# Second attention: folding three of four denominators with accumulating DMAs, and moving an exp table load

## The chip, the cores and the metric

One Trainium2 chip, one core. The time is that of the device, in microseconds, for one execution of the whole program; of several executions the median is given. Profiles come from one execution, taken by the hardware profiler.

## What is computed

Input `x` has shape (16, 256, 32, 32): 16 batches, 256 channels, 1024 positions. All data are float32. The reference, cut to what matters:

```python
# layer 0: attention with 4 heads of 64
xs  = x.reshape(B, C, S).transpose(0, 2, 1)
qkv = xs @ w_proj + b_proj
attn = softmax(q k^T * 64**-0.5) ; res = attn @ v
x = (res @ w_out + b_out + xs)            # residual
# layer 1: group norm, attention with 8 heads of 32, group norm, MLP
xn  = group_norm(x, gn1)
q, k, v = split(xn @ qkv_w.T)             # 8 heads of 32
attn = softmax(q k^T * 32**-0.5 + phys_bias) ; out = attn @ v
x = x + out @ proj_w.T + proj_b
h = gelu(mlp_w1 @ group_norm(x, gn2) + b1) ; x = x + mlp_w2 @ h + b2
```

A softmax is computed without subtracting a maximum: the exponentials are weighted with v and summed, and the result is then multiplied by the inverse of the sum of the exponentials, the denominator. The bias of a head is a constant, so its exponential is a factor: it is multiplied into the weights of v (`scale_v`, L209) and into the ones that sum the denominators (`eones`, L202).

## The kernel before, in words

The 16 batches are pipelined. For each batch the program first runs the attention of layer 0 (`attention_a`), then the hidden layer of the MLP of the batch before (`mlp`, its list `hidden`), then the attention of layer 1 (`attention_b`), and between the steps of `attention_b` it places pieces of other work: the second half of q, k, v of this attention, the projections of the next batch's first attention, and the output products of the last MLP (`fill`, L1134 to L1155).

Layouts: keys or channels lie on the 128 partitions, 512 queries (`TB`) along the free axis. `attention_b` (L508) has four items: two blocks of queries times two groups of four heads of 32, in the order of L513. An item has eight blocks of 128 keys, taken two at a time, so a step (`units`, L515) is one pair. A step computes scores for four heads and two key blocks (`scores`, L518: 16 matmuls of 32 rows by 64 columns, L532), exponentials on ScalarE (L547), on VectorE the running sum of the exponentials over the key blocks (`add`, L553, tiles `es`, two per item with two heads each, L563), and for the step before the products with v (`weigh`, L579, L584), whose result goes to `res` by ScalarE or VectorE (L595, L597).

After the last key block of an item, the sums still lie on 128 partitions, each head with 128 x 512 values. `normalise` (L601) sums over the partitions on TensorE: four matmuls of 128 rows by 32 columns (L606), one for each head, with 512 queries each. The float32 matmul is two passes, so the profile shows eight records. Each head's denominator then stands on 32 partitions. `denominators` (L357) copies them to SBUF (L358), spreads 4 x 512 values over 128 partitions by a DMA (L363), inverts them (L367), writes them to DRAM (L368) and broadcasts them back with four DMAs (L373); `scale` (L629) multiplies `res` by them, and for the second group of heads issues the projection (`out_proj`).

The order is written out by hand. Each engine runs its own instructions in the order in which they were emitted, apart from small moves by the scheduler. `Later` (L31) holds functions due after a number of ticks; the driver `run` (L1036) ticks once a step, before the step's pieces, except past the last step. The numbers in `later.after(n, ...)` are such ticks: a denominator is due at the tick of the step that weighs the item's last pair (L599), its inverse one tick later, its use one more. In `run_pieces` (L1045) each piece is followed by a tick.

PSUM has three wide tiles of two banks (`wide`, L297), handed out least recently used first, and two single banks (`bank`, L303). The scores of the first key block of a step take both single banks; `weigh` takes bank 0 and the denominators bank 1. `aside` (L307) lends a single bank to a piece of q, k or v at the start of `attention_b`.

q, k and v of `attention_b` come from `qkv` (L769): TensorE products, copied to SBUF by ScalarE (L782 for q and k, L800 for v). ScalarE uses one table set for Exp and another for Gelu, so its table is loaded at the first Gelu of a batch (L919) and at the first Exp after it (L547).

At the start of the program GpSimd loads the MLP weights, forms sums of them and keeps them in DRAM (`make_blocks`, L148). Later it has the small sums of denominators and inverses (L369, L370), which at the end decide whether all of them were in range, and one power per group norm (L746). SP issues all other DMAs.

Of the kernel before, what the change touches and what calls it, by code (L numbers as in the profile page):

```python
# [8 lines left out]
F32 = mybir.dt.float32  # L9
I32 = mybir.dt.int32  # L10
AF = mybir.ActivationFunctionType
ALU = mybir.AluOpType
AX = mybir.AxisListType

P = 128
# [3 lines left out]
HEADS1, D1 = 8, 32  # L19
TB = 512  # L20
# [34 lines left out]
def kernel(  # L55
# [21 lines left out]
    nc = tc.nc  # L77
# [8 lines left out]
    const = ctx.enter_context(tc.tile_pool(name="const", bufs=1))  # L86
# [113 lines left out]

    ebias = const.tile([P, HEADS1], F32, name="ebias")
    eones = const.tile([P, HEADS1, D1], F32, name="eones")  # L202

    def exp_bias():
        nc.scalar.activation(ebias, pb, AF.Exp)
        nc.vector.tensor_copy(eones, ebias.unsqueeze(2).to_broadcast([P, HEADS1, D1]))


    def scale_v():  # L209
# [9 lines left out]
    with ExitStack() as first:  # L219
        first_pass(  # L220
            first, tc, x, out,
            dict(
                wp=wp, bqk=bqk, pb=pb, bo=bo, g1w=g1w, g1b=g1b, g2w=g2w,
                g2b=g2b, pjb=pjb, m1b=m1b, m2b=m2b, wo=wo, wq=wq, wpj=wpj,
                m2b2=m2b2, gavg=gavg, mhalf=mhalf, ones=ones, eones=eones,
                bvo=bvo, at_start=at_start, load_rest=load_rest, exp_bias=exp_bias,
                scale_v=scale_v,
                make_blocks=make_blocks,
                in_range=in_range,
            ),  # L230
        )
# [15 lines left out]
def first_pass(ctx, tc, x, out, k):  # L247
    nc = tc.nc
# [54 lines left out]
    def bank(name, n):  # L303
        return ps_a.tile([P, TB], F32, tag=f"b{n}", name=name)
# [4 lines left out]
    def single(name):  # L309
        return bank(name, aside.pop()) if aside else wide(name)[:, 0, :]  # L310
# [43 lines left out]

    def denominators(key, den, d, full, waits, then):  # L357
        nc.scalar.copy(d, den)  # L358
        n = full.shape[1]
        w = 4 * TB // P  # L360
        spread = work.tile([P, w], F32, tag="spread", name=f"sp_{key}", bufs=2)
        row = dram.tile([4 * TB // n, n], F32, tag="row", name=f"row_{key}", bufs=4)
        nc.sync.dma_start(spread, d[::32].rearrange("p (a b) -> p a b", b=w))  # L363

        def invert():
            inverse = work.tile([P, w], F32, tag="inverse", name=f"inv_{key}", bufs=2)
            tc.keep_in_program_order(nc.vector.reciprocal(inverse, spread))  # L367
            nc.sync.dma_start(row.rearrange("r (a b) -> (r a) b", b=w), inverse)  # L368
            nc.gpsimd.tensor_add(dsum, dsum, spread)  # L369
            nc.gpsimd.tensor_add(isum, isum, inverse)  # L370
            num = P * n // (4 * TB)
            for r in range(P // num):
                nc.sync.dma_start(  # L373
                    full[r * num : (r + 1) * num], row[r].partition_broadcast(num)
                )
            later.after(waits[1], lambda: then(full))

        later.after(waits[0], invert)
# [129 lines left out]
    def attention_b(b, qT, kT, v, project):  # L508
# [70 lines left out]
        def weigh(i, kb, es):  # L579
            t, c = items[i]  # L580
            acc = bank(f"acc_{key}_{i}_{kb}", 0)
            for m in range(2):
                for g in range(G):
                    nc.tensor.matmul(  # L584
                        acc[g * D : (g + 1) * D, :],
                        v[:, kb + m, c * G + g],
                        es[2 * m + g // 2][:, g % 2, :],
                        start=(m == 0),
                        stop=(m == 1),
                    )  # L590
            if t not in res:
                res[t] = result(t)
            r = res[t][c]
            if kb == 0:
                nc.scalar.copy(r, acc)  # L595
            else:
                nc.vector.tensor_add(r, r, acc)  # L597
            if kb == SB - 2:
                later.after(1, lambda: normalise(i, r, i == len(items) - 1))  # L599

        def normalise(i, r, last):  # L601
            t, c = items[i]
            at_end = last and b == B - 1
            den = bank(f"den_{key}_{i}", 1)
            for g in range(G):
                nc.tensor.matmul(  # L606
                    den[g * D : (g + 1) * D, :],
                    k["eones"][:, c * G + g],
                    sums[i][g // 2][:, g % 2, :],
                    start=True,  # L610
                    stop=True,
                )
            full = work.tile([P, TB], F32, tag="full", name=f"rd_{key}_{i}", bufs=1)
            if at_end:

                nc.vector.reciprocal(full, den)
                scale(i, r, last, full)
                for tot, what in ((dsum, den), (isum, full)):
                    part = small.tile([P, 1], F32, tag="part", name="part")
                    nc.vector.tensor_reduce(part, what, AX.X, ALU.add)  # L620
                    nc.gpsimd.tensor_add(tot[:, :1], tot[:, :1], part)
                return
            denominators(
                f"{key}_{i}", den, full, full,
                (3, 5) if last else (1, 1),
                lambda full: scale(i, r, last, full),
            )

        def scale(i, r, last, full):  # L629
            t, c = items[i]  # L630
            tc.keep_in_program_order(nc.vector.tensor_mul(r, r, full))
            if c == CC - 1:
                issue = project(t, res[t])
                if last and b + 1 < B:
                    handed.append(issue)
                else:
                    later.after(1, issue)
# [131 lines left out]
    def qkv(key, D, src, weights, b_qk, qT, kT, v_dst):  # L769
        def qk(ch, which, t):  # L770
            ps = single(f"qk_{key}_{ch}_{which}_{t}")
            for cc in range(CC):
                product(
                    ps,
                    weights(cc, which)[:, ch * P : (ch + 1) * P],
                    src[:, cc, t * TB : (t + 1) * TB],
                    start=(cc == 0),
                    stop=(cc == CC - 1),
                )
            d = (kT if which else qT)[:, ch, t * TB : (t + 1) * TB]  # L780
            if b_qk is None:
                nc.scalar.copy(d, ps)  # L782
            else:
                nc.scalar.activation(  # L784
                    d, ps, AF.Identity, bias=b_qk[:, which, ch : ch + 1]
                )

        def v(n):
            ps = single(f"v_{key}_{n}")
            for i in range(2):  # L790
                sb = 2 * n + i
                for cc in range(CC):
                    product(
                        ps[:, i * C : (i + 1) * C],
                        src[:, cc, sb * P : (sb + 1) * P],
                        weights(cc, 2),
                        start=(cc == 0),
                        stop=(cc == CC - 1),
                    )
            nc.scalar.copy(  # L800
                v_dst()[:, 2 * n : 2 * n + 2],
                ps.rearrange("p (b h d) -> p b h d", b=2, d=D),
            )

        return (
            [
                lambda ch=ch, which=which, t=t: qk(ch, which, t)
                for ch in range(CC) for which in (1, 0) for t in range(NT)
            ],
            [lambda n=n: v(n) for n in range(SB // 2)],  # L810
        )

# [82 lines left out]
    def mlp(b, xb):  # L895
# [44 lines left out]
            gelu(0, 1, i, ps[:, 1, :])  # L940

        def finish(i):
            ps = open_sums.pop(i)
            products_of(i, [(7, ps[:, 0, :], False), (6, ps[:, 1, :], False)])
            rest = gs[1, 1, i]
            nc.vector.tensor_add(unit(0, 0, i), rest, ps[:, 0, :])  # L946
            nc.vector.tensor_add(rest, rest, ps[:, 1, :])
            gelu(0, 0, i, gs[0, 0, i])
            gelu(1, 1, i, rest)
            combine((1, 0), (0, 0), False, i)  # L950
            combine((0, 1), (1, 1), False, i)

        hidden = [
            lambda part=part, i=i: part(i)
# [4 lines left out]
        def combine(to, what, plus, only=None):  # L959
            for i in range(n4) if only is None else (only,):  # L960
                d = gs[(*to, i)]
                (nc.vector.tensor_add if plus else nc.vector.tensor_sub)(  # L962
                    d, d, gs[(*what, i)]
                )
# [128 lines left out]

    later.after(2, fold_bias)
    later.after(8, k["scale_v"])
    hidden, outputs = [], []
    last = NT * CC * SB // 2 - 1
    for b in range(B):
# [379 lines left out]
```

## Time and profile before

| | |
|---|---|
| median of 3 runs | 3666.4 us (3664.72 to 3667.44) |
| profiled execution | 3666.7 us |
| its span, first to last instruction | 3664.9 us |
| mean granted TensorE clock | 0.999 |
| matmuls of the denominators, L606 | 512 records, 67.4 us busy |
| table loads at the first Exp, L547 | 15, 1283 ns each |
| table loads at the first Gelu, L919 | 16, 1283 ns each |
| DMA over the span | 138.36 MB, mean 38 GB/s |

A busy time is the union of the intervals of an engine's instructions. Matmuls overlap each other, since each of four tiles of the array works by itself, so the duration of one record (592 ns for 512 columns) says less than the distance between the starts of two groups. "PEld" is the loading of weights, which runs beside the matmuls. A row of the timeline has the start, the duration, the engine, the line, the operation, what it writes and reads, and its count; in brackets stands how long the engine had been idle before it and what ended that. DMAs appear under the queue that issues them (SPq, or POOL for GpSimd), with the time of the issue alone, not that of the transfer.

### The profile page before, as it was taken

What the parts mean: (1) busy time and instruction counts of PE and PEld (TensorE: products, weight loads), DVE (VectorE), ACT (ScalarE), POOL (GpSimd) and SP (SyncE); (2) the same over time, 40 slices, a digit from 0 to 9 for tenths busy, and PEclk for the clock granted to TensorE, in tenths of its full rate; (3) what the DMA queues carried; (4) which work ended last, traced back from release to release, by engine and by line L of the source; (5) the groups of instructions that cost most, each with busy time, mean ns of one, the idle gap of its engine ahead of it and who ended that gap; (6) DMA issues with size and microseconds to landing.
All of it is one profiled execution on the core that took longest, in us unless ns stands there. A gap on an engine that the chain in (4) does not pass through costs nothing.

```text
span 3664.9 us, 79373 instructions
## 1 busy us (share of the span) xinstructions
PE 3632.6 (99%) x34221; PEld 1346.2 (37%) x34221; DVE 2658.1 (73%) x3424; ACT 2154.3 (59%) x2832; POOL 129.5 (4%) x266
## 2 busy tenths in 40 slices
PE   9999999999999999999999999999999999999999
PEld 3433343333433334333343333434334343343433
DVE  4586777767777677776767777677777777767777
ACT  4665657556565655656556565564655656556572
POOL 3000000000000000000000000000000000000000
PEclk9999999999999999999999999999999999999999
DMA  4000110101101011010110101101011010100100
GB/s 147 10 17 29 55 33 14 51 30 54 33 14 51 30 54 33 14 51 31 53 33 20 51 27 51 33 19 50 27 51 33 19 50 29 50 33 31 47 28 27
DMA packets 66549, 138.36 MB, mean 38 GB/s; under 512 B 35630, under 2 KB 36398, under 8 KB 61966
## 3 DMA queue, kind: packets, MB, share of 16 engines
q1 hardware_dynamic: 63116, 126.64, 10.7%
q8 instruction: 270, 4.42, 0.5%
q0 software_dynamic: 1328, 6.17, 0.5%
q14 instruction: 89, 0.73, 0.1%
q10 hardware_dynamic: 1746, 0.40, 0.1%
HBM read 111.17 MB, written 21.23 MB: 36 GB/s over the span
## 4 chain that ended last, share of the span: by engine, by line
PE 91%; DVE 4%; ACT 3%; DMA 1%; issue 1%; SPq 0%; ACTq 0%; POOL 0%; DVEq 0%
PE s_a L398 12%; PE acc_b L584 12%; PE s_b L532 12%; PE acc_a L419 12%; PE m L344 10%; PE m L906 9%; PE qk_a L344 6%; PE qk_b L344 5%; PE v_a L344 3%; PE j L344 3%; PE v_b L344 2%; ACT e_b L547 2%; PE o L344 2%; PE den_b L606 1%; DVE g L962 1%
## 5 line engine op out<-in xcount | busy, mean ns | idle before, releaser
L563 DVE TENSOR_TENSOR es_b<-es_b,e_b 128x1024 f32<-128x1024 f32 x768 | 899.3, 1219 | 243.8 <-ACT e_b L547 243.8
L547 ACT ACTIVATE e_b<-s_b 128x1024 f32<-128x1024 f32 (+1 forms) x1280 | 982.9, 864 | 132.2 <-PE s_b L532 132.0
L406 ACT ACTIVATE e_a<-s_a 128x1024 f32<-128x1024 f32 x512 | 521.2, 1025 | 360.0 <-PE s_a L398 347.6
L398 PE MATMUL s_a<-q,k 64*64 64x512 f32 x4096 | 544.3, 593 | 0.0
L419 PE MATMUL acc_a<-e_a,v 64*64 64x512 f32 x4096 | 540.1, 589 | 0.0
L532 PE MATMUL s_b<-q,k 32*64 32x512 f32 x8192 | 519.7, 600 | 4.9 <-DVE res_b L597 1.6
L431 DVE TENSOR_TENSOR es_a<-es_a,e_a 128x1024 f32<-128x1024 f32 x384 | 473.9, 1234 | 64.8 <-ACT e_a L406 41.2
L584 PE MATMUL acc_b<-e_b,v 128*32 128x512 f32 x4096 | 492.1, 598 | 0.0
L344 PE MATMUL m<-g,w 128*32 128x512 f32 (+1 forms) x3320 | 404.3, 592 | 0.0
L532 PEld LDWEIGHTS s_b<-q,k 32*64 32x64 f32 x8192 | 170.9, 130 | 321.3 <-issue 130.9
L419 PEld LDWEIGHTS acc_a<-e_a,v 64*64 64x64 f32 x4096 | 187.9, 133 | 251.5 <-issue 218.4
L398 PEld LDWEIGHTS s_a<-q,k 64*64 64x64 f32 x4096 | 175.9, 133 | 246.7 <-issue 193.1
L563 DVE TENSOR_TENSOR es_b<-e_b,e_b 128x1024 f32<-128x1024 f32 x128 | 150.8, 1220 | 153.4 <-ACT e_b L547 153.4
L906 PE MATMUL m<-gn_h,w 128*128 128x512 f32 x512 | 243.7, 604 | 5.7 <-DVE g L932 3.3
L584 PEld LDWEIGHTS acc_b<-e_b,v 128*32 128x32 f32 x4096 | 108.5, 109 | 357.5 <-ACT e_b L547 194.7
L344 PE MATMUL qk_a<-x,wp 128*32 128x512 f32 (+1 forms) x1856 | 235.1, 593 | 4.1 <-ACT k L784 4.1
L344 PE MATMUL qk_b<-gn_g,wq 128*32 128x512 f32 (+1 forms) x1280 | 234.0, 592 | 0.0
L597 DVE TENSOR_TENSOR res_b<-res_b,acc_b 128x512 f32<-128x512 f32 x192 | 131.8, 686 | 129.8 <-PE acc_b L584 129.8
L344 PEld LDWEIGHTS m<-g,w 128*32 128x32 f32 (+1 forms) x3320 | 121.4, 112 | 262.3 <-issue 235.3
L962 DVE TENSOR_TENSOR g<-g,g 128x512 f32<-128x512 f32 x320 | 206.3, 681 | 4.0 <-ACT g L919 2.8
L906 PE MATMUL m<-hs,w 128*128 128x512 f32 x384 | 177.9, 592 | 0.1
L919 ACT ACTIVATE g<-g,m1b 128x512 f32<-128x512 f32 x128 | 92.2, 722 | 99.3 <-DVE g L946 72.2
(147 smaller groups left out, 2803.6 us busy)
## 6 DMA issues: line engine op xcount, KB each, us to landing
w<-w_kept SPq DMA_DIRECT2D x30, 1792.0 KB
d_a<-row_a SPq DMA_DIRECT2D x64, 256.0 KB
rd_b<-row_b SPq DMA_DIRECT2D x252, 64.0 KB
out_dram<-x SPq DMA_DIRECT2D x63, 256.0 KB
x<-in_x_dram SPq DMA_DIRECT2D x30, 512.0 KB
w_kept<-w_made POOLq DMA_DIRECT2D x2, 1792.0 KB, 6.0
w_made<-in_L_conv_mlp_w_dram POOLq DMA_DIRECT2D x8, 256.0 KB, 6.1
x<-in_x_dram SPq DMA_DIRECT2D x4, 256.0 KB
```

The lines of the kernel that those rows point to most:

```text
L344: nc.tensor.matmul(o[sl], w[:, sl], r, **flags)
L398: nc.tensor.matmul(s[h : h + HALF, g, :], kT[g * D : (g + 1) * D, c, kb * P + h : kb * P + h + HALF], qT[g * D : (g + 1) * D, c, t * TB : ...
L406: nc.scalar.activation(e, s, AF.Exp, scale=float(D) ** -0.5)
L419: nc.tensor.matmul(accs[i][h][g * D : (g + 1) * D, :], v[h * HALF : (h + 1) * HALF, kb, c * 2 + g], e[h * HALF : (h + 1) * HALF, g, :], st ...
L431: nc.vector.tensor_add(sums[i], held[i] if kb == 1 else sums[i], e)
L532: nc.tensor.matmul(outs[g][h : h + HALF, :], kT[g * D : (g + 1) * D, c, k0 : k0 + HALF], qT[g * D : (g + 1) * D, c, t * TB : (t + 1) * TB] ...
L547: nc.scalar.activation(to, s, AF.Exp, scale=float(D) ** -0.5)
L563: ins = nc.vector.tensor_add(d, es[n % 2] if kb == 0 else d, es[n])
L584: nc.tensor.matmul(acc[g * D : (g + 1) * D, :], v[:, kb + m, c * G + g], es[2 * m + g // 2][:, g % 2, :], start=(m == 0), stop=(m == 1),)
L597: nc.vector.tensor_add(r, r, acc)
L906: nc.tensor.matmul(ps, blocks[1][number - 1][:, i * P : (i + 1) * P], inputs[b][number], start=first, stop=True, skip_group_check=not first,)
L962: (nc.vector.tensor_add if plus else nc.vector.tensor_sub)(d, d, gs[(*what, i)])
```

## The change

It has three parts.

First, the denominators of the first three items of each `attention_b` are computed in another way; the last item keeps `normalise`. As soon as the sums of an item are complete, `fold` adds the four blocks of 32 partitions of each head's sums to one another. It does so in DRAM: SP writes the first block of 32 rows (two DMAs, one for each pair of heads), and GpSimd issues three rounds of two DMAs that add the other blocks onto it. One more DMA of GpSimd loads the result as `packed`, in which the 32 rows of four heads lie on 128 partitions. Two ticks later `normalise_folded` runs four matmuls on it, of 128 rows by 32 columns, each over 128 of the 512 queries. Their weights `folded` hold, for each head, its factor in the eight columns that belong to that head and zeros elsewhere, so one matmul gives all four heads. `fold_ones` makes them on GpSimd at the start. `denominators` gets an argument `parts` for the new layout; its broadcasts go out in pieces of 128 values rather than rows of 512.

Second, the first piece of v in `attention_b` is copied by VectorE rather than ScalarE.

Third, after the last hidden piece of the MLP a small Exp on 128 x 1 values is issued on ScalarE, two ticks later.

```diff
+    folded = const.tile([P, HEADS1 * D1 // P, D1], F32, name="folded")
...
+    def fold_ones():
+        nc.gpsimd.memset(folded, 0.0)
+        g_num = P // D1
+        w = D1 // g_num
+        for c in range(HEADS1 // g_num):
+            for g in range(g_num):
+                rows = slice(g * D1, (g + 1) * D1)
+                nc.gpsimd.tensor_copy(
+                    folded[rows, c, g * w : (g + 1) * w], eones[rows, c * g_num + g, :w]
+                )
...
-    def denominators(key, den, d, full, waits, then):
+    def denominators(key, den, d, full, waits, then, parts=1):
...
-        nc.sync.dma_start(spread, d[::32].rearrange("p (a b) -> p a b", b=w))
+        nc.sync.dma_start(
+            spread, d[:: 32 // parts].rearrange("p (a b) -> p a b", b=w)
+        )
...
-                nc.sync.dma_start(
-                    full[r * num : (r + 1) * num], row[r].partition_broadcast(num)
-                )
+                to, of = full[r * num : (r + 1) * num], row[r]
+                if parts > 1:
+                    to = to.rearrange("p (n q) -> p n q", n=parts)
+                    of = row.rearrange("r (a q) -> (r a) q", a=parts).rearrange(
+                        "(n g) q -> g n q", n=parts
+                    )[r]
+                nc.sync.dma_start(to, of.partition_broadcast(num))
...
             if kb == SB - 2:
-                later.after(1, lambda: normalise(i, r, i == len(items) - 1))
+                if i == len(items) - 1:
+                    later.after(1, lambda: normalise(i, r, True))
+                else:
+                    fold(i, r)
+
+        def fold(i, r):
+            kept_sums = dram.tile(
+                [G, D, TB], F32, tag="sums", name=f"sums_{key}_{i}", bufs=2
+            )
+            by_row = kept_sums.rearrange("g p q -> p g q")
+            for j in range(G):
+                rows = slice(j * D, (j + 1) * D)
+                for n in range(G // 2):
+                    to, of = by_row[:, 2 * n : 2 * n + 2], sums[i][n][rows]
+                    if j == 0:
+                        nc.sync.dma_start(to, of)
+                    else:
+                        nc.gpsimd.dma_start(to, of, accum_op=ALU.add)
+            packed = work.tile([P, TB], F32, tag="packed", name=f"packed_{key}_{i}", bufs=1)
+            nc.gpsimd.dma_start(packed, kept_sums.rearrange("g p q -> (g p) q"))
+            later.after(2, lambda: normalise_folded(i, r, packed))
+
+        def normalise_folded(i, r, packed):
+            c = items[i][1]
+            q = TB // G
+            den = bank(f"den_{key}_{i}", 1)[:, :q]
+            for n in range(G):
+                nc.tensor.matmul(
+                    den[n * D : (n + 1) * D, :], k["folded"][:, c],
+                    packed[:, n * q : (n + 1) * q], start=True, stop=True,
+                )
+            full = work.tile([P, TB], F32, tag="full", name=f"rd_{key}_{i}", bufs=1)
+            denominators(
+                f"{key}_{i}", den, full[:, :q], full, (1, 1),
+                lambda full: scale(i, r, False, full), G,
+            )
...
         def v(n):
+            copy = nc.vector.tensor_copy if not n and b_qk is None else nc.scalar.copy
...
         def finish(i):
+            if i == n4 - 1:
+                later.after(2, back_to_exp)
...
+        def back_to_exp():
+            one = small.tile([P, 1], F32, tag="part", name=f"one_{b}")
+            nc.scalar.activation(one, gs[1, 1, n4 - 1][:, :1], AF.Exp, scale=0.0)
...
     later.after(8, k["scale_v"])
+    later.after(9, k["fold_ones"])
```

More of the change, by code (lines that the diff above doesn't have):

```diff
@@ L226 @@
                 bvo=bvo, at_start=at_start, load_rest=load_rest, exp_bias=exp_bias,
-                scale_v=scale_v,
+                scale_v=scale_v, fold_ones=fold_ones, folded=folded,
                 make_blocks=make_blocks,
@@ L623, in normalise @@
             denominators(
-                f"{key}_{i}", den, full, full,
-                (3, 5) if last else (1, 1),
-                lambda full: scale(i, r, last, full),
+                f"{key}_{i}", den, full, full, (3, 5), lambda full: scale(i, r, last, full)
             )
@@ L799, in v @@
                     )
-            nc.scalar.copy(
+            copy(
                 v_dst()[:, 2 * n : 2 * n + 2],
```

## The prediction

> **What bounds the kernel now.** I read the page first (busy shares, then the chain that ended last), then the timeline of one second-attention stretch, then the waits of TensorE.
>
> ```profile
> PE 3632.6 (99%) x34221; PEld 1346.2 (37%) x34221; DVE 2658.1 (73%) x3424; ACT 2154.3 (59%) x2832; POOL 129.5 (4%) x266
> PE 91%; DVE 4%; ACT 3%; DMA 1%; issue 1%; SPq 0%; ACTq 0%; POOL 0%; DVEq 0%
> ```
>
> TensorE's instruction stream is the time: 91% of the chain that ended last, and almost no idle. So whatever shortens TensorE's stream is gained in full, and whatever makes TensorE wait is lost in full, since its queue runs in order. GpSimd (POOL) and the DMA queues are nearly empty. The timeline around one denominator of the fourth batch (start, duration, engine, line, operation):
>
> ```profile
> 854.29 1.97 PE L532 MATMUL s_b<-q,k 32*64 32x512 f32 x32
> 858.79 3.49 DVE L563 TENSOR_TENSOR es_b<-es_b,e_b 128x1024 f32<-128x1024 f32 x3
> 861.48 1.97 PE L532 MATMUL s_b<-q,k 32*64 32x512 f32 x32
> 865.12 1.04 PE L606 MATMUL den_b<-es_b,eones 128*32 128x512 f32 x8
> 869.54 1.97 PE L532 MATMUL s_b<-q,k 32*64 32x512 f32 x32
> 871.44 1.92 PE L584 MATMUL acc_b<-e_b,v 128*32 128x512 f32 x16
> 873.18 3.62 PE L344 MATMUL m<-g,w 128*32 128x512 f32 x32
> ```
>
> A step of the second attention (scores, sums of the step before, a piece of other work) lasts 861.48 - 854.29 = 7.19 us; the one with a denominator 869.54 - 861.48 = 8.06. A denominator costs TensorE 0.87 us. VectorE has the sums it needs at 858.79 + 3.49 = 862.28, 2.8 us before TensorE asks. At the entry to a second attention:
>
> ```profile
> 320.00 1.97 PE L532 MATMUL s_b<-q,k 32*64 32x512 f32 x32
> 320.72 1.28 ACT L547 ACT_TABLE_LOAD   x1
> 322.66 1.93 PE L344 MATMUL v_b<-wq,gn_g 128*32 128x256 f32 x32 [0.68 <-ACT e_b L547]
> ```
>
> ```profile
> PE v_b L344 <- ACT e_b L547: 10.2, 15, 0.7
> ```
>
> The first exp waits for a table load, and TensorE waits for the bank that this exp empties: 15 times, 10.2 us in all.
>
> **What the Trainium skill says.** (1) "DMA: Bandwidth & Descriptors", Anatomy of one DMA: a DMA issued from GpSimd takes about 2.0 us plus bytes / 436e3, most of the fixed part being the receipt for the last byte. This trace agrees roughly:
>
> ```profile
> 26.36 0.57 POOL L161 DMA_DIRECT2D w_kept<-w_made  x1 [0.30 <-POOL w_made L157]
> 32.93 3.02 POOL L152 DMA_DIRECT2D w_made<-in_L_conv_mlp_w_dram  x4 [6.00 <-DMA w_kept<-w_made]
> ```
>
> From the issue to the instruction that waited for it are 6.57 us for 1,835,008 bytes (1792 KB); taking 4.21 for the bytes leaves 2.36 us fixed, with the wake-up. (2) The same page, Rules for kernel authors: an accumulating DMA reads its destination and writes it later, so the next access must wait for its semaphore. No run yet shows one; but it makes the added DMAs a series. (3) "ScalarE: Activation LUTs", What ACT_TABLE_LOAD costs: 1283 ns plus a drain of about 1380. The trace shows 1.28 us, and the first exp follows at once: the trace decides.
>
> **The change, part by part.** The sum is made against the profiled execution, 3666.7 us (span 3664.9), 0.3 above the median of 3666.4.
>
> *Shorter denominators.* 48 of 64 go from 512 to 128 columns, still two passes of four tiles. The trace has no 128-column wave; it has 256-column ones: v_b's 32 matmuls run from 330.03 to 331.75, 0.215 us a wave. Half of it, 0.11, is the lower bound, 0.215 the upper; the four weight loads of a wave take 0.13, which I take: 2 x 0.13 = 0.26 us, saving 0.61 (0.44 to 0.65). In the 14 middle batches that is 42 x 0.61 = 25.6 us (18 to 27). In the first and last batch steps have little other work and scores wait for exps (2.85 instead of 1.97 us), so 6 denominators there save nothing. ScalarE's copy (0.63 us) shrinks too, off the path.
>
> *The fold that feeds them.* For each of the 48: two plain DMAs on SP (each 131 KB to DRAM), then on GpSimd three rounds of two accumulating DMAs, then one DMA that loads 262 KB into `packed`. Each round waits for the round before, in the same bytes; the two halves run beside each other. The denominator's matmuls wait for `packed`, and behind them in TensorE's queue stands everything. Length of the series, from the later half's last add (862.28):
> - the plain write: SP's 8 KB row write goes from 876.60 to the DMA that waits for it at 878.12, 1.52 us; plus 0.28 for the bytes, 1.8;
> - three accumulating rounds: 2.36 + 0.30 = 2.66 each, 7.98 (an unmeasured kind; below: the page's 2.3 each; above: bytes moved three times, source, destination and back, 3.26 each);
> - `packed`: 2.36 + 0.60 = 2.96 (below 2.6).
>
> Sum 12.7 us; 11.3 with the lower prices, 14.5 with the upper. The time there is for it: the new place is one step later, after that step's acc. That is 873.18, less the 0.87 of the denominator that has left the step before: 872.31. So 872.31 - 862.28 = 10.0 us. TensorE stands 2.7 us (1.3 to 4.5) in each of 42: 113 us (55 to 189). In the first and last batch a step takes only about 5 us: sums ready at 175.46, next acc issued by 181.24, 5.8 us there; the stall is 6.9 less about 1 us that ScalarE would have made TensorE wait anyway: 6 x 5.9 = 35 us (27 to 46). Nothing hides it: TensorE has no other queue.
>
> *Exp table in the gap.* The load moves ahead of a copy of k at 314.95, delaying that copy about 1.5 us; its reader is the score matmul at 320.00, so 2.9 us cover it. v[0] goes to VectorE, idle 9.38 us there, about 0.7 us. What goes is 322.66 - 320.00 = 2.66 against 328.28 - 326.38 = 1.90 in the next step, 0.76, and 0.14 in the restart of the scores: 0.9 x 15 = 13 us (10 by the waits alone; below that if the bank comes free late for another reason). In the last batch the load is added for nothing, in ScalarE's idle time.
>
> *At no cost, and why.* `fold_ones`: nine small GpSimd operations ahead of the weight sums of the start, whose result is first read some 200 us later. SP: its two writes wait for VectorE, and output stores and the spread stand behind them; stores have a whole batch. Broadcasts in 512-byte pieces: four issues took 1.71 to 2.63 us and have a whole step of 7.19 us. GpSimd's queue: behind the waiting DMAs stand the dsum and isum adds, later by some us and read at the end; the group norm's power is not behind a fold. The projection of the first half moves one step later, in front of the last denominator: same work in another order, below 1 us a batch. `es` buffers are taken again four steps later, 29 us, over twice the series. DMA volume: 48 x 1.3 MB at a mean of 38 GB/s now, no limit.
>
> Sum: -25.6 - 13 + 113 + 35 = +109: 3776 us. With the lower prices +55 + 27 - 27 - 13 = +42, 3709; with the upper, and 10 (the waits' 10.2) for the table, 189 + 46 - 18 - 10 = +207, 3874.
>
> **Rivals.** *The series fits (ends faster).* Mechanism: the fixed part of a GpSimd DMA, f. The series is 3.3 + 4f; with f as short as SP's 1.52 it is 9.4 us, inside 10.0, and only the first and last batch stall, 6 x 2.6 = 16: 3666.7 - 25.6 - 13 + 16 = 3644, down to 3630 if those are covered too. It decides from f = 1.68 down; break-even is f about 1.78. For it: the only single GpSimd DMA in the profile is fourteen times larger, so its fixed part may hold descriptor work that a small one lacks. Against: even the page's 2.0 is too long. *Balance:* f near 1.8, stalls of 0.4 to 0.6 us eat the gains: 3660 to 3675. *Much longer:* accumulation in DRAM over 4 us a round, series 17 us and more; 42 x 6.8 + 6 x 10 - 38 = +308, 3975; nothing in the profile speaks for it, nothing excludes it.
>
> **Chances.** Stall as costed 0.57; fits 0.28; balance 0.06; much longer 0.09. About 0.2% (7 us) can be told from no change. So faster 0.28, same 0.06, slower 0.66. The likeliest gives 3776, its own range 3709 to 3874. The range over all must reach down to the rival that fits: 3630 to 3880.
>
> **What would show it.** In the profile after: TensorE's idle before den_b put down to the DMA of `packed`, near 2.7 us times 42 and more in the first and last batch; GpSimd's accumulating issues 2.7 us apart; den_b steps otherwise 0.6 us shorter; no table load at the first exp and v_b's wait gone. If den_b follows acc_b without idle, the fixed part was mis-sized and the rival holds. If table loads go but v_b still waits, the 13 us are wrong.

## The result, and the profile after

| | before | after |
|---|---|---|
| median | 3666.9 us (4 runs) | 4070.3 us (4 runs, 4068.4 to 4073.9) |
| span of the profiled execution | 3664.9 us | 4066.6 us |
| mean granted TensorE clock | 0.999 | 0.955 |

The change makes the kernel slower: ratio 1.110, interval [1.1083, 1.1121], 403 us. The forecast was 3776 us, its range 3630 to 3880. The direction and the place were right; the size was not.

The page of the kernel after, its busy row and its chain of what ended last:

```profile
PE 3718.7 (91%) x34221; PEld 1371.0 (34%) x34221; DVE 2678.4 (66%) x3440; ACT 2135.4 (53%) x2833; POOL 399.0 (10%) x611
...
PE 68%; DMA 19%; DVE 7%; issue 4%; POOL 1%; SPq 0%; ACT 0%; POOLq 0%; DVEq 0%; ACTq 0%
```

TensorE was 99% busy and is 91% busy. Its busy time has also grown, by 86 us, although the change takes columns away from it: the same matmuls run more slowly somewhere. In the chain, DMAs went from 1% to 19%. Where TensorE waits is one line of its waits (total us, times, longest):

```profile
PE den_b L645 <- DMA packed_b<-sums_b: 325.1, 48, 9.9
```

All 48 folded denominators wait for their sums. One of them, in the timeline of a middle batch (start, duration, engine, line, operation; in brackets the idle time before and what ended it):

```profile
924.00 3.49 DVE L582 TENSOR_TENSOR es_b<-es_b,e_b 128x1024 f32<-128x1024 f32 x3
926.38 1.44 SPq L633 DMA_DIRECT2D sums_b<-es_b  x2
928.89 0.87 POOL L635 DMA_DIRECT2D sums_b<-es_b  x1 [7.76 <-DVE x L1080]
929.96 0.83 POOL L635 DMA_DIRECT2D sums_b<-es_b  x1 [0.20 <-DVE g L1021]
932.24 0.83 POOL L635 DMA_DIRECT2D sums_b<-es_b  x1 [1.45 <-DMA sums_b<-es_b]
933.26 0.83 POOL L635 DMA_DIRECT2D sums_b<-es_b  x1 [0.19 <-issue]
935.53 0.83 POOL L635 DMA_DIRECT2D sums_b<-es_b  x1 [1.44 <-DMA sums_b<-es_b]
935.78 1.92 PE L603 MATMUL acc_b<-e_b,v 128*32 128x512 f32 x16
936.55 0.83 POOL L635 DMA_DIRECT2D sums_b<-es_b  x1 [0.19 <-issue]
940.23 0.61 POOL L637 DMA_DIRECT2D packed_b<-sums_b  x1 [2.85 <-DMA sums_b<-es_b]
943.29 0.65 PE L645 MATMUL den_b<-packed_b,folded 128*32 128x128 f32 x8 [5.59 <-DMA packed_b<-sums_b]
943.69 5.67 PE L357 MATMUL m<-g,w 128*32 128x512 f32 x32
```

The sums are ready at 927.49, where the additions of VectorE end (924.00 + 3.49). The three rounds of the later half go out at 929.96, 933.26 and 936.55, so 3.3 us apart here, and the load of `packed` follows 3.7 us after the last. TensorE has issued acc by 937.7 and starts the denominator at 943.29. Then comes what the forecast did not have: the 32 matmuls `m` behind it take 5.67 us, where the same group took 3.62 before. The clock by stretches (span of the stretch, busy times, then PEclk, DMA share, GB/s) tells why: first and third are such groups behind a wait, the second is one without a wait.

```profile
943.70:949.30 5.60, 5.60 (x41) 1.39 (x31) 2.08 (x3) 0.27 (x1) 0.21 (x1) 0.63 0.03 4
960.12:963.60 3.48, 3.48 (x36) 0.91 (x28) 3.23 (x4) 1.32 (x2) 0.00 (x0) 1.00 0.24 71
980.87:986.60 5.73, 5.73 (x39) 1.52 (x31) 0.00 (x0) 0.27 (x1) 0.21 (x1) 0.61 0.03 4
```

After a wait of 5.6 us the granted clock is 0.63 for the next 5.6 us. That is itself a mean. The same place, cut where the granted clock changes:

```profile
937.57:940.98 3.41, 0.13 (x4) 0.00 (x0) 3.18 (x3) 1.74 (x3) 0.61 (x1) 1.00 0.41 60
940.98:944.39 3.41, 1.10 (x12) 0.66 (x16) 0.00 (x0) 0.27 (x1) 0.00 (x0) 0.50 0.24 82
944.39:947.81 3.42, 3.42 (x20) 0.90 (x16) 1.09 (x2) 0.00 (x0) 0.21 (x1) 0.50 0.03 2
947.81:951.22 3.41, 3.41 (x52) 1.00 (x44) 2.79 (x5) 1.39 (x3) 0.00 (x0) 1.00 0.00 0
```

The clock is either full or half. It halves within the wait, at 940.98, and is full again at 947.81, 4.5 us after the denominator has started. In the traces of all the kernels here, every stretch at half clock that ends within the program lasts 3.41 us or a multiple of it, and within one trace all of them start on one grid of that step. After a grid step at full clock in which TensorE was busy for less than 0.38 of the time (in the first row above 0.13 of 3.41 us), half clock followed in all 116 cases; after one with more than 0.65 it never did; in between both occurred. The mean of 0.955 over the span is made of 48 such places and a short one at each end of the program.

The entry to a second attention, after:

```profile
361.49 1.97 PE L551 MATMUL s_b<-q,k 32*64 32x512 f32 x32
361.60 0.69 DVE L853 COPY v<-v_b 128x512 f32<-128x512 f32 x1 [4.54 <-PE v_b L357]
363.40 1.93 PE L357 MATMUL v_b<-wq,gn_g 128*32 128x256 f32 x32
```

From the scores to `v_b` it is 1.91 us now, 2.66 before, with no idle in brackets: this part works as meant.

**Where the 403 us are.** Compared step by step (start of one step's scores to the start of the next) with the kernel that lacks only the fold (first experiment), the 14 middle batches differ at the places of the folded denominators and nearly nowhere else. The step that used to hold the denominator is 0.86 us shorter, in all 42 cases. The step that now holds it is longer by 7.7 to 11.7 us. Summed over the trace: waits ahead of the 42 denominators 282 us (6.7 each, over the normal distance of two groups), the slow group behind each 78 us (1.9 each), the shorter denominators themselves -19; the first and last batch together +68, of which 52 are their six waits; the work between the attentions +5; the entry -13. That is +401, against 401.7 between the spans.

### The profile page after: what moved, and what is told of

Its sections match the earlier page's. It is cut to its first block, busy times and chain, and to the rows that moved or that the text cites. A ratio compares the mean times of both kernels' runs of the same rounds, so it can differ in the third digit from the quotient of the medians.

```text
span 4066.6 us, 80283 instructions
## 1 busy us (share of the span) xinstructions
PE 3718.7 (91%) x34221; PEld 1371.0 (34%) x34221; DVE 2678.4 (66%) x3440; ACT 2135.4 (53%) x2833; POOL 399.0 (10%) x611
## 4 chain that ended last, share of the span: by engine, by line
PE 68%; DMA 19%; DVE 7%; issue 4%; POOL 1%; SPq 0%; ACT 0%; POOLq 0%; DVEq 0%; ACTq 0%
DMA sums_b<-es_b 13%; PE s_a L417 11%; PE acc_a L438 11%; PE s_b L551 7%; PE acc_b L603 7%; PE m L959 6%; PE m L357 6%; PE qk_b L357 5%; PE qk_a L357 4%; DMA packed_b<-sums_b 3%; DVE es_b L582 3%; PE j L357 3%; PE v_b L357 3%; PE v_a L357 2%; PE o L357 1%
## 5 line engine op out<-in xcount | busy, mean ns | idle before, releaser
L551 PE MATMUL s_b<-q,k 32*64 32x512 f32 x8192 | 529.8, 604 | 4.3 <-DVE res_b L616 1.7
L357 PE MATMUL m<-g,w 128*32 128x512 f32 (+1 forms) x3320 | 458.4, 660 | 0.0
L635 POOL DMA_DIRECT2D sums_b<-es_b x288 | 242.0, 848 | 1109.8 <-DMA sums_b<-es_b 970.1
L645 PE MATMUL den_b<-packed_b,folded 128*32 128x128 f32 x384 | 31.4, 417 | 325.1 <-DMA packed_b<-sums_b 325.1
L357 PE MATMUL qk_a<-x,wp 128*32 128x512 f32 (+1 forms) x1856 | 262.1, 655 | 3.8 <-ACT k L836 3.8
L357 PEld LDWEIGHTS m<-g,w 128*32 128x32 f32 (+1 forms) x3320 | 136.7, 125 | 285.1 <-issue 261.7
L371 ACT COPY rd_b<-den_b 128x128 f32<-128x128 f32 (+1 forms) x63 | 21.6, 342 | 345.0 <-PE den_b L645 287.3
```

Of the source, the lines that this page charges most:

```text
L357: nc.tensor.matmul(o[sl], w[:, sl], r, **flags)
L551: nc.tensor.matmul(outs[g][h : h + HALF, :], kT[g * D : (g + 1) * D, c, k0 : k0 + HALF], qT[g * D : (g + 1) * D, c, t * TB : (t + 1) * TB] ...
L635: nc.gpsimd.dma_start(to, of, accum_op=ALU.add)
```

## The experiments

All ratios are to the kernel before, timed beside each on the same chip. The kernels are told as edits of the kernel after.

**1. No fold.** Parts two and three of the change alone; all denominators by `normalise`.

```diff
             if kb == SB - 2:
-                if i == len(items) - 1:
-                    later.after(1, lambda: normalise(i, r, True))
-                else:
-                    fold(i, r)
+                later.after(1, lambda: normalise(i, r, i == len(items) - 1))
...
-                f"{key}_{i}", den, full, full, (3, 5), lambda full: scale(i, r, last, full)
+                f"{key}_{i}", den, full, full, (3, 5) if last else (1, 1),
+                lambda full: scale(i, r, last, full),
```

> The change without the fold: all four denominators as before, v[0] on VectorE and the early Exp kept. Theory (the fold alone makes the loss; the other two parts bring 0.9 us at each of 15 entries): 3667 - 13.5 = 3653 us, with v_b no longer waiting at the entry. Rival (the moved table load or the copy on VectorE also costs, hidden in the total): 3667 or more.

Measured: 3654.6 us, ratio 0.9964 [0.9952, 0.9976], 13 us faster than before. The first step of a second attention takes 5.49 us in place of 6.37, 0.88 in each batch: the 0.9 of the forecast. So the whole loss, and 13 us more, is the fold's.

**2. The Exp alone.** As 1, with `v[0]` copied by ScalarE again.

```diff
-            copy = nc.vector.tensor_copy if not n and b_qk is None else nc.scalar.copy
+            copy = nc.scalar.copy
```

> Third part of the change alone: no fold, v[0] copied by ScalarE as before, dummy Exp in the gap. Theory of the prediction's sum (the table load is what made TensorE wait at the entry; the copy of v[0] only follows it): as fast as with both parts, 3654.6, within 2 us. Rival (without the copy on VectorE the copy of v[0] stands in ScalarE's queue behind the exps and holds a bank): part of the 12 us stays, 3658 to 3667.

Measured: 3652.8 us, ratio 0.9964 [0.9951, 0.9978]: the same as 1. The dummy Exp is worth the 13 us; moving the copy of `v[0]` as well is worth nothing that can be measured (moving it alone was not tried).

**3. TensorE kept busy while it waits.** Seven matmuls that nobody reads, put into TensorE's queue ahead of each folded denominator; the fold is untouched.

```diff
             q = TB // G
+            keep_warm(k["wq"][:, 0, :TB], 7)
             den = bank(f"den_{key}_{i}", 1)[:, :q]
```

> The changed kernel with seven 128x128x512 matmuls, whose result nobody reads, ahead of each folded denominator, about 6 us of work in a wait that is 6.1 to 10.4 us long. Theory (after the wait TensorE runs for some us at a lower granted clock, 32 matmuls then take 5.4 instead of 3.4 us): the clock stays up, 48 x 2.0 = 96 us go, 3975 us (3960 to 3995). Rival (the work after the wait is slow because of something else, DMA traffic or the copy of the denominators): no gain, 4070 or more.

Measured: 3986.9 us, ratio 1.0869 [1.0852, 1.0885]; 83 us less than the change. The mean clock is 0.997. In the middle batches, the 32 matmuls behind a denominator take 3.5 to 3.6 us again, and the denominators still come as late, 17.0 us after the sums are ready (16.7 in the change). Step by step in the two traces, the 42 middle places are 85 us shorter from the denominator on (78 for the groups behind, 7 for the denominators themselves) and 10 us longer ahead of it; in the first and last batch five of six keep the half clock, and little changes. So the low clock is a cost of its own, added to the wait.

**4. Plain writes for accumulating ones.** GpSimd issues the same DMAs, but each round overwrites; the additions over the blocks are left out, so the denominators are not the reference's.

```diff
-                        nc.gpsimd.dma_start(to, of, accum_op=ALU.add)
+                        nc.gpsimd.dma_start(to, of)
```

> The changed kernel with plain writes in place of the accumulating ones, same queue, same waits; the additions are left out, so the denominators are those of the last 32 rows. Theory (accumulation itself makes a round longer: 3.55 us instead of the 2.66 that I reckoned): rounds of about 2.7 us, 3 x 0.9 x 48 = 130 us less wait, 3940 us. Rival (the fixed part of a GpSimd DMA and the spacing of two issues of 1.1 us make the round, whatever the DMA does to the bytes): 4035 to 4070.

Measured: 3947.9 us, ratio 1.0762 [1.0746, 1.0779], 122 us less than the change. The page's list of DMAs (KB each, median us from issue to landing), first of the change, then of this kernel:

```profile
sums_b<-es_b POOLq DMA_DIRECT2D x288, 128.0 KB, 3.1
```

```profile
sums_b<-es_b POOLq DMA_DIRECT2D x288, 128.0 KB, 2.2
```

The same bytes from and to the same places land in 2.2 us when they are written and in 3.1 when they are added. Averaged over the middle batches, from the later half's issue to its next: rounds of 3.69, 3.53 and 3.76 us in the change, 2.93, 2.67 and 2.96 here. Addition costs 0.8 us a round. Part of it is in the issue: GpSimd is busy for 0.85 us with an accumulating DMA, 0.54 with a plain one (page, mean of 288). The DMA packets in the two traces show the rest. For the DMAs issued while no other GpSimd DMA of the fold was in flight (49 and 52, medians), the first packet starts 1.46 us after the issue with addition and 1.15 without, and the landing follows 1.65 and 1.12 us after that, in packets of 2 KB with addition and 4 KB without. So some 0.3 us lie ahead of the transfer and 0.5 in it.

**5. All by SP, plain.** As 4, with every DMA of the fold on SP. The Trainium skill ("DMA: Bandwidth & Descriptors", SWDGE vs HWDGE vs iDMA) says that accumulation goes from GpSimd alone; no run here tries it from SP, and the additions are left out here too.

```diff
-                    if j == 0:
-                        nc.sync.dma_start(to, of)
-                    else:
-                        nc.gpsimd.dma_start(to, of, accum_op=ALU.add)
+                    nc.sync.dma_start(to, of)
...
-            nc.gpsimd.dma_start(packed, kept_sums.rearrange("g p q -> (g p) q"))
+            nc.sync.dma_start(packed, kept_sums.rearrange("g p q -> (g p) q"))
```

> All DMAs of the fold issued by SP as plain writes, the load of the packed sums too; the additions over the blocks are left out, so the denominators are not those of the reference. Theory 'the price of a hop is GpSimd's': SP's hops take about 1.9 us, the series is 4 x 1.9 + 2.3 = 9.9 us, about the 10.0 there is, and only the first and last batch stall: 3640 to 3680. Rival 'a write of 131 KB to DRAM and its receipt take 2.5 us whoever issues it': series about 12.5 us, stall 2.5 x 48 plus the cold clock: about 3790. By GpSimd, plain, it was 3947.9.

Measured: 3733.7 us, ratio 1.0182 [1.0167, 1.0198]: between the two theories. One fold of it:

```profile
861.08 1.44 SPq L632 DMA_DIRECT2D sums_b<-es_b  x2
...
863.82 5.17 SPq L632 DMA_DIRECT2D sums_b<-es_b  x6
...
870.67 0.34 SPq L634 DMA_DIRECT2D packed_b<-sums_b  x1
...
873.55 0.43 PE L642 MATMUL den_b<-packed_b,folded 128*32 128x128 f32 x8 [1.15 <-ACT e_b L566]
...
873.77 3.64 PE L357 MATMUL m<-g,w 128*32 128x512 f32 x32
```

Rounds are 2.1 to 2.2 us by SP, the load 2.8, the series 11.4 us (means of the middle batches). That is 1.4 longer than the time there is. The wait of 1.15 us here leaves the group `m` behind it at 3.64: no low clock. (The bracket names an exp, but in the trace `packed` lands at 873.42, just before the denominator starts.) In this run 40 of the 48 places kept the full clock; the eight that did not stood behind waits of 2.3 to 5.3 us, and three others of 2.3 to 2.6 us slowed nothing. No shorter wait slowed a group in it.

**6. Later place, two items.** Only the first two items of the 14 middle batches are folded, and their denominators are due one step later, where the place is about 17 us after the sums.

```diff
-                if i == len(items) - 1:
-                    later.after(1, lambda: normalise(i, r, True))
+                if i > 1 or b in (0, B - 1):
+                    later.after(1, lambda: normalise(i, r, i == len(items) - 1))
...
-            later.after(2, lambda: normalise_folded(i, r, packed))
+            later.after(3, lambda: normalise_folded(i, r, packed))
```

(With the second hunk of experiment 1.)

> Only the first two items of the 14 middle batches are folded, and their denominators are due one step later (three ticks): 10.0 + 7.2 = 17.2 us for a series that took 15.8 to 19.0, 16.7 on average. Theory (the loss is TensorE's wait for the series and nothing else of the fold): 3653 - 28 x 0.61 + 28 x 0.3 = 3644 us (3636 to 3655). Rival (the fold's DMAs also cost by their traffic or by holding GpSimd and SP): 3670 or more though TensorE hardly waits for the packed sums.

Measured: 3654.0 us (3650.6 to 3661.3), ratio 0.9960 [0.9946, 0.9974]. Better than before, but by no more than experiment 1, which has no fold at all. The forecast gain of 10 us over it did not come. The profiled run, at the slow end of these, has 16 of 28 denominators at their place within 0.2 us, the others 0.3 to 3.2 late, and two of these with slow groups behind them: the series varies by several us from batch to batch.

**7. Later place, plain writes.** As 6, with the edit of 4 (additions left out): a shorter series in the same place.

> Two items of each of the 14 middle batches folded, due one tick later than in the change, with plain writes in place of the accumulating ones (the additions over the blocks are left out, so these denominators are not those of the reference): a series of 13.5 us in a place of about 17, so that no wait is left and the time is that of 28 shorter denominators. By the prediction's 0.61 each: 3654.6 - 17 = 3637.5. If a denominator of 128 columns costs nearly what its rows in the trace after show with the pauses beside it (0.5 us in place of 0.26): 3644. Rival (the shorter denominator gains nothing, since scores wait for exps or banks instead): 3654.

Measured: 3641.0 us, ratio 0.9929 [0.9915, 0.9942], 13.6 us below experiment 1. The two steps of a folded denominator are 8.05 and 7.19 us without the fold, 7.19 and 7.41 with it: 0.64 us gained each, a little over the forecast's 0.61. 28 x 0.64 = 17.9; some 4 us of it come back in another step, which 9 explains.

**8. A shorter series.** As 6, but SP writes two blocks to two places, one round adds the other two, one DMA from DRAM to DRAM adds the second place to the first.

```diff
-                    if j == 0:
+                    if j < 2:
                         nc.sync.dma_start(to, of)
...
+            nc.gpsimd.dma_start(
+                kept_sums.rearrange("g p q -> (g p) q"),
+                kept[1].rearrange("g p q -> (g p) q"), accum_op=ALU.add,
+                max_dma_last_dim=512,
+            )
```

> Two items of each of the 14 middle batches folded, due one tick later than in the change, with a shorter series: SP writes blocks 0 and 1 to two places, one round of four accumulating DMAs adds blocks 2 and 3 to them, one more accumulating DMA from DRAM to DRAM adds the second place to the first, then the load. By the rounds measured (1.9 and 1.1 for SP's second pair, 3.5 and 2.2 for two more issues of GpSimd, 3.5, 3.1) the series is about 15 us in a place of 16.6 to 17.2, so that it comes in time in nearly all batches: as fast as the plain writes in that place, 3641 to 3646. Rival (an accumulation from DRAM to DRAM, whose both sides are in DRAM, is slower than one from SBUF, or the jitter of the transfers is what is late): no faster than the folds of three rounds in that place, 3650 or more.

Measured: 3705.2 us, ratio 1.0103 [1.0086, 1.012]. A miss. The addition between two places in DRAM, of 262 KB, takes 5.14 us here to the load that waits for it:

```profile
811.79 1.07 POOL L638 DMA_DIRECT2D sums_b<-sums_b  x1 [2.95 <-DMA sums_b<-es_b]
816.93 0.60 POOL L644 DMA_DIRECT2D packed_b<-sums_b  x1 [4.07 <-issue]
820.94 0.40 PE L652 MATMUL den_b<-packed_b,folded 128*32 128x128 f32 x8
```

The first items still come in time in 13 of 14 batches. The second items do not: the last of SP's four writes goes out 2.9 to 4.9 us after the second there, not 0.85, and the fourth addition 7 us or more after it. SP's queue shows what stands in front of that write (the last row):

```profile
832.89 0.34 SPq L383 DMA_DIRECT2D row_b<-inv_b  x1
833.28 0.89 SPq L634 DMA_DIRECT2D sums_b<-es_b  x2
834.38 1.77 SPq L394 DMA_DIRECT2D rd_b<-row_b  x4
836.20 0.51 SPq L634 DMA_DIRECT2D sums_b<-es_b  x1
```

It is the store of the first item's inverse and the four broadcasts that wait for it. In the later place they fall into the second item's fold.

**9. Only the first item, and where the gain goes.** As 6 and as 8, with `if i > 0 or b in (0, B - 1)`: 14 denominators folded.

> As the run with two items folded in the later place, by the change's own series of three rounds, but only the first item of each of the 14 middle batches: 14 shorter denominators at 0.64 each are 9 us, the second items' waits are gone, and the copy of the third denominator no longer waits for the buffer of the second's inverse. The first item's series was late there in 5 of 14 batches, about 3 us and 1.7 of low clock. Theory: 3654 - 9 + 0 to 5 = 3645 to 3650. Rival (the jitter of the series costs what it gains): 3652 to 3656.

> The same with the shorter series (one round of four additions, one addition from DRAM to DRAM), which came in time for the first item in 12 of 14 batches: 3645 to 3647. Rival as above: 3652 to 3656.

Measured: 3658.5 us, ratio 0.9974 [0.9965, 0.9984], and 3659.1, 0.9977 [0.9968, 0.9985]: 4 us slower than no fold and outside all that was expected, though the lateness of the fold adds up to only 3 us over the 14 batches in either trace. Without it they would stand where no fold stands, not 9 us below. So the gain itself is missing. The steps show 0.64 gained at the folded denominator and 0.66 or more lost later in every batch, 0.82 on average (11.5 in all). The place, in the first of the two:

```profile
834.32 1.04 PE L660 MATMUL den_b<-es_b,eones 128*32 128x512 f32 x8
...
837.99 0.68 DVE L684 TENSOR_TENSOR res_b<-res_b,rd_b 128x512 f32<-128x512 f32 x1
838.72 2.63 PE L551 MATMUL s_b<-q,k 32*64 32x512 f32 x32
838.75 0.59 ACT L371 COPY rd_b<-den_b 128x512 f32<-128x512 f32 x1 [0.92 <-DVE res_b L684]
```

The second item's long denominator is ready at 835.4, but ScalarE's copy of it starts at 838.75, as soon as VectorE has used the first item's inverse (837.99 + 0.68). Both use the one buffer `full`. Behind the copy in ScalarE's queue stand the exps, so the scores take 2.63 us in place of 1.97. In the later place, the first item's inverse is used in the same step in which the next item wants the buffer.

**10. The buffer's step back.** As 9 (three rounds, one item) and as 6 (two items); the long denominator that follows a folded one is due one step later.

```diff
-                    later.after(1, lambda: normalise(i, r, i == len(items) - 1))
+                    late = 2 if i == 1 and 0 < b < B - 1 else 1
+                    later.after(late, lambda: normalise(i, r, i == len(items) - 1))
```

(`i == 2` for two items.)

> As the run with the first item alone folded (three rounds, later place), but the second item's denominator, which stays long, is asked for one step later, after the first item's inverse has been used. Theory: what took the gain back is one buffer; the copy of the second denominator waits in ScalarE's queue for the tile that still holds the first item's inverse, and the exps behind it and the scores wait with it, 0.66 us a batch. Then 3658.5 - 14 x 0.66 = 3649, less if some of the late series come in time. Rival (the delay belongs to the later place of the folded item itself): 3656 to 3660.

> As the run with two items folded (three rounds, later place), but the third item's denominator is asked for one step later. Theory as above: the third step's delay of 0.1 to 0.56 us a batch goes, 3654.0 - 4 = 3650, with the jitter of the second items' series left (3646 to 3657). Rival: no change, 3654.

Measured: 3647.3 us, ratio 0.9946 [0.9932, 0.9960], and 3648.3, 0.9949 [0.9936, 0.9963]. These are the fastest kernels here that compute everything, 20 and 19 us below before. The first of them at the same place:

```profile
835.05 1.97 PE L551 MATMUL s_b<-q,k 32*64 32x512 f32 x32
...
838.70 1.04 PE L661 MATMUL den_b<-es_b,eones 128*32 128x512 f32 x8
...
840.32 0.66 ACT L371 COPY rd_b<-den_b 128x512 f32<-128x512 f32 x1
...
843.10 1.97 PE L551 MATMUL s_b<-q,k 32*64 32x512 f32 x32
```

The copy follows the denominator without idle in brackets, and the scores of both steps take 1.97. 14 x 0.66 = 9.2 us were expected back, 11.2 came, near the 11.5 that the steps showed lost. The theory of the buffer holds; a second buffer, the more direct test, was not tried. Against no fold, 14 shorter denominators are now worth 7.3 of the 9.0 us that 14 x 0.64 make; with two items, 6.3 of 17.9 are left (6.6 and 5.6, when each is taken against the kernel before that was timed beside it). In that trace the lateness of the series adds up to 10.9 us, and 1.8 for slow groups behind it, about what is missing.

## Why the prediction was wrong, point by point

*The bound and the place.* Right. TensorE's stream is the time. The time between ready sums and the new place was put at 10.0 us; it is 16.73 - 6.72 = 10.0 in the means of the 42 middle folds. All 48 denominators wait; the next longest wait of TensorE adds up to 4.2 us.

*The series.* The first failed step. Its terms in the means of the middle batches:

| | forecast | measured |
|---|---|---|
| SP's write to the first addition | 1.8 | 2.67 |
| three additions | 3 x 2.66 (bounds 2.3 and 3.26) | 3.69 + 3.53 + 3.76 |
| load of `packed` | 2.96 | 3.08 |
| sum | 12.7 | 16.7 |

"Three accumulating rounds: 2.36 + 0.30 = 2.66 each" is what a plain GpSimd DMA of these bytes takes at best (2.67 to 2.96, experiment 4); the addition is 0.8 more, and 3.66, the mean of the three, stands even over the upper bound. That bound counted bytes three times and left the fixed part as it was. So the error was to take the size of an unmeasured kind from its bytes. The write's term came from one SP DMA of 8 KB; SP's own next DMA follows the write of 131 KB at 2.1 us (experiment 5), an addition of GpSimd at 2.5 in the median, and at 2.7 on average because of a few late ones. It is 2.5 for the first half of the sums too (926.38 to 928.89 in the fold shown), ahead of which GpSimd had been idle for 7.76 us, so its queue is not the reason. That the two halves run beside each other was right: in either half an addition goes out 0.3 us after the landing of the one before, on average, and the halves are 1.1 us apart because SP's two writes are.

*The wait.* In the middle batches 42 x 2.7 = 113 was forecast, 282 measured: all of the 4.0 us that the series is longer arrive at TensorE. In the first and last batch 5.9 each was forecast, 8.6 measured.

*The clock.* The second failed step, and one that was left out: the sum took a wait to cost its own length. Experiment 3 shows some 85 us in the middle batches that come on top. The Trainium skill has it ("TensorE: Matmul & The Clock Gate", What's actually happening and Why this matters for your kernels): an idle window of about 3.4 us throttles the array to half its clock, the window runs freely, and idle gaps over about 3 us are to be avoided. From that page, an estimate: 3.4 us at half clock lose 1.7 us; the trace has 1.9 a wait. The traces agree with a free-running window: it is the grid of 3.41 us in the section on the result. They differ in how idle it must be, since windows in which TensorE was busy for up to 0.38 of the time halved the clock as well. So it depends on where a wait lies on the grid: the shortest that slowed the work behind it lasted 2.15 us, the longest that did not 3.16 (both in experiment 8). The 2.15 lies below the page's 3, and the measurement decides. At the forecast's 2.7 the price was due in a part of the cases, at its 5.9 for the first and last batch, and in the rival "much longer", in all; it was missing.

*The sum.* Of the 294 us between 3776 and the result, the longer waits of the middle batches make 282 - 113 = 169, the slow groups behind them 78, the denominators at the low clock 7, the first and last batch (waits, low clock and the rest) 68 - 35 = 33, the work between the attentions 5.

*Shorter denominators.* Right as a term: 0.61 forecast, 0.64 measured where there is no wait (experiment 7). In the change only 0.45 each, since they run at the low clock: start to the next group 0.40 us in place of 0.22.

*The Exp.* Right: 13 forecast, 13 measured (experiment 1), and the dummy Exp alone has it (experiment 2).

*What was put at nothing.* GpSimd's queue, SP's writes, the broadcasts, `fold_ones` and the DMA volume cost nothing that shows: the steps away from the folded denominators are the same to 0.01 us in most middle batches. `es` buffers and the later projection likewise.

*The rivals.* "The series fits" needed a fixed part of 1.68 us or less. Rounds by SP take 2.1 to 2.2 with their bytes and the series 11.4, so it fails even there. "Much longer" named the mechanism, accumulation as the unknown, with 4 us a round; 3.66 were measured. Its 3975 us is near what the change takes without the low clock (3986.9, experiment 3).

Open: why the transfer of an addition takes 0.5 us longer than that of a write (its reading of the destination and its smaller packets were not separated), and why the series varies by several us from batch to batch.

## What to carry to other kernels

A series of dependent DMAs is priced per hop, from issue to the next issue that waits for it, and a kind of DMA that no trace shows needs a run of its own, not a bound from its bytes. Where TensorE is the bound, a wait costs its length and, in each place where it is long enough, about 2 us of low clock behind it: here none below 2.15 us did so, those up to 3.16 us in some cases, and all longer ones. When a step is moved later, look also for the buffer that it then holds longer: here one shared tile took back all that a shorter denominator gained, and one step's delay of the next user returned it.

## What the runs showed that I had not expected

- An accumulating GpSimd DMA of 131 KB from SBUF to DRAM takes 3.5 to 3.8 us on average from its issue to the issue that waits for it, a plain one 2.7 to 3.0, one by SP 2.1 to 2.2. An accumulating one of 262 KB from DRAM to DRAM took 5.1 us in the fold shown.
- An accumulating GpSimd DMA goes out 0.3 us after the landing of the one it waits for, on average, and keeps GpSimd busy for 0.83 us.
- The granted clock is full or half, and half in stretches of 3.41 us or its multiples, on one grid per run.
- Behind a wait of 5.6 us, 32 matmuls took 5.67 us in place of 3.62, at a granted clock of 0.63. Behind one of 1.15 us they took 3.64.
- A matmul wave of 128 columns on four tiles costs 0.11 us of TensorE's stream, half of the 0.215 of a 256-column wave: two passes add 0.22 us to a step.
